# A graph network layer on one Trainium2 core: row beginnings by selection matrices, and the first count matrix made between the normalisations of x

## The chip, the cores and the metric

The kernel runs on one core of one Trainium2 chip. The time is device microseconds of one execution. Before the change the median of three runs is 3082.79 us (3079.99 to 3087.31). A profile is one further execution, taken by the hardware profiler; its own time stands beside it.

The engines are PE (matrix products; PEld is its weight load), DVE (vector), ACT (activations), POOL (GpSimd) and SP (issues DMAs). Each takes its instructions in order.

## The reference

6250 nodes with 256 features, and 100000 edges (src, dst), sorted by dst. x is normalised per row and clipped at zero, goes through four graph layers, and is added to the result:

```python
h = jnp.maximum(_layernorm(x, axis=-1), 0.0)
deg = segment_sum(ones, dst)
h = h @ W1_self + (segment_sum(h[src], dst) / clip(deg, 1)) @ W1_neigh + b1     # mean
hp = relu(h @ W2_pool + b2_pool)                                                # pool
h = h @ W2_self + segment_max(hp[src], dst) @ W2_neigh + b2
h = ((segment_sum(h[src], dst) + h) / (deg + 1)) @ W3_neigh + b3                # gcn
h = h @ W4_self + (segment_sum(h[src], dst) / clip(deg, 1)) @ W4_neigh + b4     # mean
return x + (h @ W_fc + b_fc)
```

dst is drawn as 6250 u^2, so the first nodes have many edges.

## The kernel before, in words

The nodes are 49 tiles of 128. Edges of tiles 8 to 48 are summed in `sums`: for each block of 128 edges one indirect DMA on POOL gathers 128 rows of a table (L379) into a ring of 14, a one-hot of the edges' node (`hot`, L375, DVE) is the weight of three matmuls (L397; a row is stored as three bf16 parts), and groups of four blocks are added to tiles on DVE (L414, L416). There are 474 such gathers in the first layer.

Tiles 0 to 7 (18 in later layers) have so many edges that they are done as a dense product with a **count matrix** A: how many edges lead from each node to each of the 128 nodes of the tile. `build` makes it from windows of 8 nodes. A window has up to 31 rows of 128 edges; for each row there is a one-hot of the source's place in its tile (`hs`, 128 x 128: two ACT activations, Abs at L303 and Relu at L305), a one-hot of tile and node (`hm`, 128 x 392, DVE, L307), and one matmul (L313); ACT evicts a window to fp8 (L317). Tile 0's matrix has 139 rows, tiles 1 to 7 have 322 together. `dense` multiplies it with the rows of all 49 tiles (L435, three matmuls each). `Hub` holds the pieces of matrices and dense products; `sums` takes from it in proportion to the gathers done, and one-hots are made up to four pieces ahead (`LOOK`), in rings of seven.

Ahead of the first layer stands the **preparation**:

- `load_x` and `layer_norm`: x in seven groups of seven tiles, in three buffers. DVE makes statistics (L567, L568), ACT normalises tile by tile (L577), and the group is split in three bf16 parts: first part by ACT (L580), subtraction on DVE (L581), second part by POOL (L582), subtraction on DVE (L583). SP stores it to `tab_h` (L584), which the gathers read.
- The first edge of each window of nodes. For 384 window bounds in three columns, a first lookup of rows of dst (`drow`, L614, one buffer, three in turn) and a count (L618) give the starts (`SN`). They are turned into one row by PE (`starts`), a check (`room`, `has`) is made, and POOL copies the starts in runs to the 896 rows of the matrices with 128 times the row's number added (`at_row`, L646 and L648, 33 runs). Seven small matmuls turn this back into columns (`atI`).
- `window_rows` looks up 128 dst and 128 src per row with `atI` (L669, seven times two indirect DMAs on POOL), and PE turns them (L679). `window_keys` makes the keys `sk` and `mk` from them on DVE (L686 to L695), for the first 512 rows (tiles 0 to 7) and later for the rest.
- `products1`: products of weights, in eight steps on PE and ACT. `turn` and `tail_keys`: the keys of the summed edges.

The order within an engine is made by a scheduler from the program's order and its dependencies, so that the work of these parts is interleaved. The first layer begins with `hub.advance(first)`, which makes the matrix of tile 0, and then `sums`. As each tile is complete, `done1` multiplies it with the weights (L815 to L838) and SP stores a tile of `tab_p` (L839). The second layer's gathers (L1137, POOL) read `tab_p` and begin once the last tile is stored.

Of the kernel before, what the change touches and what calls it, by code (L numbers as in the profile page):

```python
# [73 lines left out]
def fast_path(  # L74
# [216 lines left out]
    def build(d, A, keys, pool, psb):  # L291
# [3 lines left out]
        for w in range(d * WT, (d + 1) * WT):  # L295
            hold = {}
            for k in range(k_of[w]):
# [3 lines left out]
                def hot(r=r, hots=hots):  # L301
                    t = pool.tile([P, P], BF16, name="ht", bufs=3)
                    nc.scalar.activation(t, iota_b, AF.Abs, bias=sk[:, r : r + 1])  # L303
                    hots[0] = pool.tile([P, P], BF16, name="hs", bufs=LOOK + 3)
                    nc.scalar.activation(hots[0], t, AF.Relu, bias=one, scale=-1.0)  # L305
                    hots[1] = pool.tile([P, NT * WIN], BF16, name="hm", bufs=LOOK + 3)
                    nc.vector.tensor_scalar(hots[1], iota_w, mk[:, r : r + 1], None,  # L307
                                            op0=ALU.is_equal)
# [201 lines left out]
    for d in range(H1, NT):  # L510
        last = d == NT - 1
        ends = (g_of[d][0] * G * P, EX if last else (g_of[d][1] + 1) * G * P,
                offs[b_of[d][0]], EX if last else offs[b_of[d][1] + 1])
        for k in range(4):
            nc.gpsimd.memset(lim[:, k, d : d + 1], float(ends[k]))
# [8 lines left out]
    mk1 = w1pool.tile([P, RB1], F32, name="mk1")  # L524

    with ExitStack() as pro:
# [18 lines left out]
        def load_x(g):  # L545
            xt = lp.tile([P, LG, FI], F32, name="xt", bufs=3)
# [11 lines left out]
        for g in range(3):  # L558
            load_x(g)

        def layer_norm(g):
# [19 lines left out]
            nc.vector.tensor_sub(xt, xt, hi)  # L581
            nc.gpsimd.tensor_copy(mid, xt)  # L582
# [4 lines left out]
            )  # L587

# [22 lines left out]
        drows = dflat[0:EP].rearrange("(p t) -> p t", t=T)  # L611
        for c in range(3):
            row = ep.tile([P, T], I32, name="drow", bufs=1)
            nc.gpsimd.indirect_dma_start(  # L614
                out=row, out_offset=None, in_=drows,
                in_offset=bass.IndirectOffsetOnAxis(ap=cI[:, c : c + 1], axis=0),
            )
            nc.vector.tensor_scalar(row, row, SN[:, c, 1:2], 0.0, op0=ALU.is_lt, op1=ALU.add,  # L618
                                    accum_out=within[:, c : c + 1])
        nc.vector.scalar_tensor_tensor(SN[:, :, 0], cF, float(T), within,  # L620
                                       op0=ALU.mult, op1=ALU.add)
        pr_ = bank(psm, "pm", "pr_s", (3 * P,))
        for c in range(3):
            nc.tensor.matmul(pr_[:2, c * P : (c + 1) * P], SN[:, c, :], ident,
                             start=True, stop=True)
        starts = ep.tile([2, 3 * P], F32, name="starts")
        nc.vector.tensor_copy(starts, pr_[:2, :])


        room = ep.tile([1, NW], F32, name="room")  # L630
        i = 0
        while i < NW:
            n = sum(1 for w in range(i, NW) if k_of[w] == k_of[i])
            nc.gpsimd.memset(room[:, i : i + n], float(k_of[i] * P))
            i += n
        has = ep.tile([1, NW], F32, name="hasw")
        nc.vector.tensor_sub(has, starts[:1, 1 : NW + 1], starts[:1, :NW])
        nc.vector.tensor_tensor(has, has, room, op=ALU.is_gt)
        nc.vector.tensor_reduce(bad[:1, 1:2], has, AX.X, ALU.max)


        at_row = ep.tile([2, RB * P], F32, name="at_row")
        nc.gpsimd.memset(at_row, 0.0)
        nc.gpsimd.memset(at_row[:1, :], float(E))
        for r, w0, n, k in spans:
            nc.gpsimd.tensor_copy(at_row[:, r : r + n], starts[:, w0 : w0 + n])  # L646
            if k:
                nc.gpsimd.tensor_scalar(at_row[:1, r : r + n], at_row[:1, r : r + n],  # L648
                                        float(k * P), None, op0=ALU.add)
        pa = bank(psm, "pm", "pa", (RB, 2))  # L650
        for b in range(RB):
            nc.tensor.matmul(pa[:, b, :], at_row[:, b * P : (b + 1) * P], ident[:2, :2],
                             start=True, stop=True)
        atF = ep.tile([P, RB, 2], F32, name="atF")
        nc.vector.tensor_copy(atF, pa)
        atI = ep.tile([P, RB], I32, name="atI")
        nc.vector.tensor_copy(atI, atF[:, :, 0])


        sk = ep.tile([P, RB * P], F32, name="skf")  # L660
        mk = ep.tile([P, RB * P], F32, name="mkf")
        skI = ep.tile([P, RB * P], I32, name="skI")
        dw = ep.tile([P, RB * P], F32, name="dwf")

        def window_rows(b):
            got = []
# [13 lines left out]
            c = slice(b * P, (b + 1) * P)  # L680
# [3 lines left out]
        def window_keys(c0, c1):  # L684
            c = slice(c0, c1)
# [91 lines left out]
        turn()  # L777
        for b in range(RB1 // P):
            window_rows(b)
        window_keys(0, RB1)  # L780
        nc.vector.tensor_copy(sk1, sk[:, :RB1])
        nc.vector.tensor_copy(mk1, mk[:, :RB1])
        for g in range(NT // LG):
            layer_norm(g)
            if g + 3 < NT // LG:
                load_x(g + 3)
            next(steps, None)
            if RB1 // P + g < RB:
                window_rows(RB1 // P + g)
        for _ in steps:  # L790
# [1172 lines left out]
```

## Time and profile before

| what | value |
|---|---|
| median of three runs | 3082.79 us |
| the profiled execution | 3087.14 us, span 3085.3 us, granted clock 0.907 |
| busy PE, PEld | 2456.4 us (80%), 1401.4 us (45%) |
| busy DVE, ACT, POOL | 2053.6 (67%), 893.7 (29%), 2054.0 us (67%) |
| first gather of tab_h (L379) | 147.53 us |
| first gather of tab_p (L1137) | 820.96 us |
| L305 hs, all matrices | 781 of 395 ns mean |
| L307 hm with mk | 461 of 344 ns mean |
| L581, L583 subtractions | 7 of 2.02 us, 7 of 2.01 us mean |
| L582 cast on POOL | 7 of 1.76 us mean |

How to read it: a page gives busy time of each engine, and groups of instructions by line with the idle time just before them and what ended it ("<-"). In a timeline each row has the start and the duration in us from the span's start, the engine, the line, what is written from what, how many of them were merged ("x27"), and the idle time before. POOL's rows of an indirect DMA are its issue, not its transfer.

### The profile page before, as it was taken

What the parts mean: (1) busy time and instruction counts of PE and PEld (TensorE: products, weight loads), DVE (VectorE), ACT (ScalarE), POOL (GpSimd) and SP (SyncE); (2) the same over time, 40 slices, a digit from 0 to 9 for tenths busy, and PEclk for the clock granted to TensorE, in tenths of its full rate; (3) what the DMA queues carried; (4) which work ended last, traced back from release to release, by engine and by line L of the source; (5) the groups of instructions that cost most, each with busy time, mean ns of one, the idle gap of its engine ahead of it and who ended that gap; (6) DMA issues with size and microseconds to landing.
All of it is one profiled execution on the core that took longest, in us unless ns stands there. A gap on an engine that the chain in (4) does not pass through costs nothing. (4 is left out here: it accounts for less than half of the span.)

```text
span 3085.3 us, 41397 instructions
## 1 busy us (share of the span) xinstructions
PE 2456.4 (80%) x12699; PEld 1401.4 (45%) x12699; DVE 2053.6 (67%) x5303; ACT 893.7 (29%) x2383; POOL 2054.0 (67%) x2260
## 2 busy tenths in 40 slices
PE   1568999999768555666789997972899899799997
PEld 0234666666433222232334443431344344688786
DVE  4955666655367677555789997974466667576665
ACT  2557766664255566311111111000000001000000
POOL 5274777776366776777667777764676677677663
PEclk9777999999889777788899998985999999899999
DMA  5454667776599999999989998976999999777774
GB/s 190 152 159 138 203 208 211 213 217 211 196 392 376 362 388 352 362 389 384 314 274 324 315 309 296 323 248 210 361 387 373 364 386 382 254 225 219 208 210 135
DMA packets 379984, 865.38 MB, mean 280 GB/s; under 512 B 58064, under 2 KB 151202, under 8 KB 379720
## 3 DMA queue, kind: packets, MB, share of 16 engines
q0 software_dynamic: 146560, 514.74, 50.7%
q1 hardware_dynamic: 175108, 292.47, 25.6%
q10 hardware_dynamic: 58084, 55.44, 5.6%
q8 instruction: 103, 1.69, 0.2%
q14 instruction: 129, 1.06, 0.1%
HBM read 610.65 MB, written 252.58 MB: 280 GB/s over the span
## 5 line engine op out<-in xcount | busy, mean ns | idle before, releaser
L1137 POOL DMA_INDIRECT X<-tab_p,srcIf x782 | 842.3, 1077 | 368.6 <-issue 170.5
L397 PE MATMUL pg<-ring,hot 128*128 128x256 bf16 (+2 forms) x3390 | 685.9, 311 | 96.2 <-DMA ring<-tab_h,srcT 36.5
L435 PE MATMUL pd<-zt,ac 128*128 128x256 bf16 (+1 forms) x3462 | 569.9, 300 | 36.3 <-DMA ac<-tab_a 31.1
L379 POOL DMA_INDIRECT ring<-tab_h,srcT x474 | 450.7, 951 | 194.3 <-PE pg L397 72.2
L397 PEld LDWEIGHTS <-hot 128*128 128x128 bf16 x3390 | 334.2, 99 | 332.1 <-issue 163.4
L435 PE MATMUL pd<-r,ae 128*128 128x512 bf16 x1536 | 383.4, 399 | 102.9 <-DVE acc L934 46.9
L379 POOL DMA_INDIRECT ring<-tab_r,srcE x342 | 333.0, 974 | 162.2 <-PE pg L397 72.5
L435 PEld LDWEIGHTS <-ac 128*128 128x128 fp8e4 x3462 | 338.8, 98 | 171.3 <-DMA ac<-tab_a 23.9
L379 POOL DMA_INDIRECT ring<-tab_s,srcE x314 | 297.7, 948 | 130.2 <-PE pg L397 49.4
L1142 DVE SCALAR_TENSOR_TENSOR X<-X,samef,X 128x512 f32<-128x512 f32 x385 | 288.3, 749 | 133.2 <-DMA X<-tab_p,srcIf 90.9
L416 DVE SCALAR_TENSOR_TENSOR acc<-pg,M,acc 128x257 f32<-128x257 f32 (+2 forms) x518 | 274.7, 561 | 150.6 <-PE pg L397 150.3
L1142 DVE SCALAR_TENSOR_TENSOR X<-X,samef 128x512 f32<-128x512 f32 x391 | 293.1, 750 | 114.2 <-DMA X<-tab_p,srcIf 108.0
L313 PE MATMUL pb<-hm,hs 128*128 128x392 bf16 x781 | 256.2, 376 | 132.4 <-ACT A L317 66.4
L305 ACT ACTIVATE hs<-ht,onef 128x128 bf16<-128x128 bf16 x781 | 290.2, 395 | 240.9 <-PE pb L313 221.9
L435 PEld LDWEIGHTS <-ae 128*128 128x128 fp8e4 x1536 | 156.4, 102 | 338.9 <-issue 198.8
L1219 DVE TENSOR_SCALAR_CACHE_REDUCE many<-ac 128x896 bf16<-128x896 fp8e4 (+2 forms) x144 | 138.7, 963 | 132.7 <-DMA ac<-tab_a 132.7
L1076 PE MATMUL pm_prf<-unf,hTf 128*128 128x512 f32 x392 | 203.9, 647 | 16.6 <-ACT hTf L1067 16.6
L375 DVE TENSOR_SCALAR hot<-iota_bf,keyE 128x128 bf16<-128x128 bf16 x656 | 151.2, 274 | 72.5 <-PE pg L397 65.4
L307 DVE TENSOR_SCALAR hm<-iota_w,mk 128x392 bf16<-128x392 f16 x461 | 155.2, 344 | 56.7 <-PE pb L313 55.0
L317 ACT ACTIVATE A<-pb 128x392 fp8e4<-128x392 f32 x288 | 139.8, 489 | 182.0 <-PE pb L313 137.7
L435 PE MATMUL pd<-Z,A 128*128 128x256 bf16 (+1 forms) x1176 | 187.4, 274 | 0.2
L313 PEld LDWEIGHTS <-hs 128*128 128x128 bf16 x781 | 81.4, 105 | 217.7 <-issue 89.2
(288 smaller groups left out, 2908.1 us busy)
## 6 DMA issues: line engine op xcount, KB each, us to landing
runb<-X SPq DMA_DIRECT2D x208, 512.0 KB
runb<-X SPq DMA_DIRECT2D x183, 256.0 KB
tab_r<-r SPq DMA_DIRECT2D x49, 384.0 KB
tab_a<-A SPq DMA_DIRECT2D x18, 784.0 KB
tab_t<-th SPq DMA_DIRECT2D x49, 256.0 KB
tab_p<-hpf SPq DMA_DIRECT2D x49, 256.0 KB
th<-tab_t ACTq DMA_DIRECT2D x49, 256.0 KB
X<-tab_p,srcIf POOLq DMA_INDIRECT x782
```

The costliest lines, as they stand in the source:

```text
L305: nc.scalar.activation(hots[0], t, AF.Relu, bias=one, scale=-1.0)
L307: nc.vector.tensor_scalar(hots[1], iota_w, mk[:, r : r + 1], None, op0=ALU.is_equal)
L313: nc.tensor.matmul(hold[0], hots[0], hots[1], start=(k == 0), stop=(k == k_of[w] - 1))
L317: nc.scalar.copy(A[:, :, c : c + WIN], hold[0].rearrange("p (s c) -> p s c", c=WIN), saturate=True)
L375: nc.vector.tensor_scalar(hot[j], iota_b, keyT[:, j - jb : j - jb + 1], None, op0=ALU.is_equal)
L379: nc.gpsimd.indirect_dma_start(out=ring[:, j % deep, : 3 * F], out_offset=None, in_=table, in_offset=bass.IndirectOffsetOnAxis(ap=srcT[:, ...
L397: nc.tensor.matmul(pg[:, : F + c], hot[j], X[:, part * F : (part + 1) * F + c], start=(k == 0 and part == 2), stop=(k == n - 1 and part == 1),
L416: nc.vector.scalar_tensor_tensor(acc[d], pg, m, acc[d], op0=ALU.mult, op1=ALU.add)
L435: nc.tensor.matmul(hold[0][:, : F + c], a, z[:, part * F : (part + 1) * F + c], start=(s == ss[0] and part == 2), stop=(s == ss[-1] and pa ...
L1076: nc.tensor.matmul(pm, hT[:, c, :], un[:, c, :], start=False, stop=(c == KH - 1))
L1137: nc.gpsimd.indirect_dma_start(out=X[:, k, :], out_offset=None, in_=tab_p, in_offset=bass.IndirectOffsetOnAxis(ap=srcI[:, t : t + 1], axis=0),
L1142: nc.vector.scalar_tensor_tensor(X[:, k, :], prev, same[:, t : t + 1], X[:, k, :], op0=ALU.mult, op1=ALU.max,)
```

## The change

It has five parts. (1) The starts are no longer turned into a row. `win_of` holds for each of the 896 rows the number of its window (33 iotas on POOL), `select` makes of it three matrices with a one where the row's window is the partition's (DVE), and a matmul of `SN` with such a matrix, plus one of `later` (128 times the row's number) with a unit row, gives the beginnings as columns. The beginnings of tiles 0 to 7 need the first lookup of dst alone; `drow` has two buffers. (2) The check moves behind the second normalisation, and the fills of `lim` behind `turn`. (3) The keys of tiles 0 to 7 are made in place. (4) In `layer_norm`, the first subtraction moves from DVE to POOL and the second cast from POOL to ACT; x has two buffers in place of three. (5) The matrix of tile 0 is made in shares between the normalisations (`made.advance`), with its `hs` by one POOL instruction each; the other matrices keep ACT's. The first layer's Hub begins without it.

```diff
@@ build @@
-    def build(d, A, keys, pool, psb):
+    def build(d, A, keys, pool, psb, other=False):
...
                 def hot(r=r, hots=hots):
-                    t = pool.tile([P, P], BF16, name="ht", bufs=3)
-                    nc.scalar.activation(t, iota_b, AF.Abs, bias=sk[:, r : r + 1])
                     hots[0] = pool.tile([P, P], BF16, name="hs", bufs=LOOK + 3)
-                    nc.scalar.activation(hots[0], t, AF.Relu, bias=one, scale=-1.0)
+                    if other:
+                        nc.gpsimd.tensor_scalar(hots[0], iota_b, sk[:, r : r + 1], 0.0,
+                                                op0=ALU.add, op1=ALU.is_equal)
+                    else:
+                        t = pool.tile([P, P], BF16, name="ht", bufs=3)
+                        nc.scalar.activation(t, iota_b, AF.Abs, bias=sk[:, r : r + 1])
+                        nc.scalar.activation(hots[0], t, AF.Relu, bias=one, scale=-1.0)
@@ before the preparation @@
+    As = [bpool.tile([P, NT, P], F8, name="A0", bufs=1)]
+    made = Hub(build(0, As[0], (sk1, mk1, 0), bpool, psb1, other=True))
@@ load_x, layer_norm @@
-            xt = lp.tile([P, LG, FI], F32, name="xt", bufs=3)
+            xt = lp.tile([P, LG, FI], F32, name="xt", bufs=2)
...
             nc.scalar.copy(hi, xt)
-            nc.vector.tensor_sub(xt, xt, hi)
-            nc.gpsimd.tensor_copy(mid, xt)
+            nc.gpsimd.tensor_sub(xt, xt, hi)
+            nc.scalar.copy(mid, xt)
             nc.vector.tensor_sub(lo, xt, mid)
@@ beginnings @@
+        for r, w0, n, k in spans:
+            nc.gpsimd.iota(win_of[:, r : r + n], pattern=[[1, n]], base=w0,
+                           channel_multiplier=0, allow_small_or_imprecise_dtypes=True)
+            nc.gpsimd.memset(later[:, r : r + n], float(k * P))
...
+        def select(c):
+            nc.vector.tensor_scalar(sel[c], win_of[:, sel_at[c] : sel_at[c] + sel[c].shape[1]],
+                                    float(-c * P), pidx, op0=ALU.add, op1=ALU.is_equal)
...
-        for r, w0, n, k in spans:
-            nc.gpsimd.tensor_copy(at_row[:, r : r + n], starts[:, w0 : w0 + n])
-            if k:
-                nc.gpsimd.tensor_scalar(at_row[:1, r : r + n], at_row[:1, r : r + n],
-                                        float(k * P), None, op0=ALU.add)
...
+        def row_begins(b0, b1, cs):
+            pa = bank(psm, "pm", "pa", (RB, 2))
+            for b in range(b0, b1):
+                for c in cs:
+                    nc.tensor.matmul(pa[:, b, :], sel[c][:, b * P - sel_at[c] : (b + 1) * P - sel_at[c]],
+                                     SN[:, c, :], start=(c == cs[0]), stop=False)
+                nc.tensor.matmul(pa[:, b, :], later[:, b * P : (b + 1) * P], unit,
+                                 start=False, stop=True)
+            nc.vector.tensor_copy(atF[:, b0:b1, :], pa[:, b0:b1, :])
+            nc.vector.tensor_copy(atI[:, b0:b1], atF[:, b0:b1, 0])
@@ the order of the preparation @@
         steps = products1()
-        turn()
+        begins(0, 1)
+        row_begins(0, RB1 // P, (0,))
         for b in range(RB1 // P):
             window_rows(b)
-        window_keys(0, RB1)
-        nc.vector.tensor_copy(sk1, sk[:, :RB1])
-        nc.vector.tensor_copy(mk1, mk[:, :RB1])
+        window_keys(sk1, mk1)
+        select(1)
+        select(2)
+        begins(1, 3)
+        row_begins(RB1 // P, RB, (1, 2))
+        turn()
...
         for g in range(NT // LG):
             layer_norm(g)
-            if g + 3 < NT // LG:
-                load_x(g + 3)
+            if g + 2 < NT // LG:
+                load_x(g + 2)
             next(steps, None)
             if RB1 // P + g < RB:
                 window_rows(RB1 // P + g)
+            made.advance(len(made.work) * (g + 1) // (NT // LG + 2))
+            if g == 1:
+                check_room()
...
+        made.advance(len(made.work) * (NT // LG + 1) // (NT // LG + 2))
@@ the first layer @@
-        builds = [build(d, As[d % 2], keys, wk, psb) for d in range(H1)]
+        builds = [None] + [build(d, As[d % 2], (sk1, mk1, 0), bpool, psb1) for d in range(1, H1)]
...
-        work = list(builds[0])
-        first = len(work)
+        work = []
         for d in range(H1):
             work += merged(denses[d], builds[d + 1]) if d + 1 < H1 else denses[d]
+        made.advance(len(made.work))
         hub = Hub(work)
-        hub.advance(first)
         todo.append(segments())
```

## The prediction

> **What bounds the kernel now.** I read first the POOL timeline from 130 to 830 us, because the change ends where the first aggregation begins. Columns: start, duration, what, and in brackets the idle time before it and what ended it.
>
> ```profile
> 147.53 0.97 POOL L379 DMA_INDIRECT ring<-tab_h,srcT  x1 [9.24 <-DMA tab_h<-Z]
> ...
> 242.74 0.99 POOL L379 DMA_INDIRECT ring<-tab_h,srcT  x1 [0.30 <-PE pb L313]
> 244.04 0.95 POOL L379 DMA_INDIRECT ring<-tab_h,srcT  x1 [0.30 <-PE pb L313]
> 268.11 0.95 POOL L379 DMA_INDIRECT ring<-tab_h,srcT  x1 [23.13 <-PE pg L397]
> 272.69 0.94 POOL L379 DMA_INDIRECT ring<-tab_h,srcT  x1 [3.62 <-PE pg L397]
> ...
> 782.35 0.94 POOL L379 DMA_INDIRECT ring<-tab_h,srcT  x1 [0.71 <-PE pg L397]
> 820.96 0.97 POOL L1137 DMA_INDIRECT X<-tab_p,srcIf  x1 [37.66 <-DMA tab_p<-hpf]
> ```
>
> The first gather waits for the last tab_h store, so the preparation ends at S = 147.5. The next stage's first gather (L1137) waits for the last tab_p row, at 821.0. Everything later stands behind that gather, so a shift of it passes to the end one for one: the kernel is as long as S, plus this stage, plus an unchanged rest. The stage lasts 673.4 us. Gathers are issued every 1.25 us, so 474 of them take 591; there is one hole of 27 us at 244 to 273, where the ring is full because PE, in order, sits in the first count matrix; and at the end PE is behind. The windows view shows the latter (PE busy, PEld, DVE, ACT, POOL, granted clock, DMA share, GB/s):
>
> ```profile
> 200.00:250.00 50.00, 32.71 (x132) 14.28 (x130) 28.21 (x99) 35.22 (x116) 34.23 (x36) 0.70 0.51 147
> 600.00:650.00 50.00, 49.74 (x321) 32.91 (x320) 28.34 (x106) 31.67 (x84) 38.10 (x40) 1.00 0.73 223
> 700.00:750.00 50.00, 49.87 (x333) 34.21 (x332) 27.79 (x98) 28.11 (x72) 33.84 (x37) 1.00 0.68 200
> ```
>
> POOL's 40 gathers per 50 us (its pace) fall to 37 once PE has no idle time left. From 200 to 250 PE has time, at clock 0.70: there it waits for one-hots from ACT.
>
> The preparation is read from the whole timeline, 38 to 76 us:
>
> ```profile
> 40.21 2.75 POOL L646 COPY at_row<-starts 2x128 f32<-2x128 f32 x4 [3.03 <-DVE starts L627]
> 47.70 7.38 POOL L648 TENSOR_SCALAR at_row<-at_row 1x19 f32<-1x19 f32 x27
> 58.45 3.81 POOL L669 DMA_INDIRECT wrow<-dflat,atI  x1 [0.66 <-DVE nb L575]
> 58.93 2.01 DVE L583 TENSOR_TENSOR Z<-xt,Z 128x1792 bf16<-128x1792 f32 x1
> ```
>
> POOL makes the row beginnings in 62 small instructions, 40 to 56 us, and the row lookups (L669) start only at 58.5.
>
> **The change, part by part.**
>
> *Row beginnings (earlier by 31).* Removed: three chained lookups before anything, the 62 POOL instructions, the transposition. Added ahead of them on POOL: 33 iotas and 33 fills over 782 elements. An iota of 392 takes 0.45 us and one of 1 takes 0.13, the 164 fills of lim 5.5 in all; that gives about 5 us of iotas and fills, after win_of is cleared on DVE at about 4. The lim fills still stand ahead of the first dflat lookup in the built order: 4.4 + 5 + 0.5 + 5.5 = 15.4, against 13.3 before. Its data took 6.9 us from issue, so 22.3; then DVE 1.03 + 0.16, eight small matmuls at 0.3, two copies with a 1.03 us count between them: row lookups at 27.3 in place of 58.5. From lookup to finished keys (L694) before took 32.6 us with casts and subtractions of x in between; without these, some 25: keys at 52.5 in place of 91.
>
> *First count matrix (moved off the stage, onto POOL).* Its 139 one-hot pairs, matmuls and 16 evictions leave the stage. On ACT a pair (Abs, Relu) cost 1.17 us for two. On POOL each is one TENSOR_SCALAR with a pointer scalar and two operations; the trace has the same kind with one operation. POOL's groups by form, mean ns behind the busy time:
>
> ```profile
> L582 POOL CAST Z<-xt 128x1792 bf16<-128x1792 f32 x7 | 12.4, 1764 | 41.0 <-DVE xt L581 41.0
> L648 POOL TENSOR_SCALAR at_row<-at_row 1x1 f32<-1x1 f32 x17 | 3.4, 198 | 1.3
> L648 POOL TENSOR_SCALAR at_row<-at_row 1x128 f32<-1x128 f32 x1 | 0.6, 554 | 0.0
> ```
>
> So 2.8 ns per element plus 0.2; I take 0.55, and 0.62 with the gap of 0.07 that the run of 27 shows. Below: 0.38, if it runs like POOL's copy of 160 elements (0.31 + 0.07). Above: 0.98, if the second operation doubles the per-element part.
>
> Here a rule of the Trainium skill speaks against the change. DVE makes the other one-hot (L307) at the same time, from the same engine port. The rows where the two meet before:
>
> ```profile
> 136.42 1.87 POOL L582 CAST Z<-xt 128x1792 bf16<-128x1792 f32 x1 [1.67 <-DVE xt L581]
> 136.68 2.89 DVE L307 TENSOR_SCALAR hm<-iota_w,mk 128x392 bf16<-128x392 f16 x6
> 141.42 3.55 DVE L307 TENSOR_SCALAR hm<-iota_w,mk 128x392 bf16<-128x392 f16 x15
> ```
>
> Fifteen alone take 3.55 (0.24 each); six begun beside POOL's cast take 2.89 in place of 1.42, and 58.45 above shows the other direction: a POOL lookup of 0.94 takes 3.81 beside DVE's two-input subtraction. The skill ("SBUF — State Buffer", section "SBUF: two separate sides") says why: VectorE and GpSimd arbitrate for one port pair, which is locked for the whole instruction, the loser waiting. By it a one-hot pair costs 0.62 + 0.24 = 0.86, not 0.62. By the row alone the 119 one-hots ahead of the fifth subtraction take 74 us, by the rule 102; the first would turn my sum to a gain of 12. I take the rule, as the trace shows both directions.
>
> *x's subtraction to POOL, the cast to ACT.* POOL has no two-input row. Below: its one-input cast, 1.7 us; above: the TENSOR_SCALAR slope, 0.2 + 1792 x 2.8 ns = 5.2. The skill ("GPSIMD Engine Reference", section "3.1 Elementwise — side-by-side cycle accounting") gives 4497 ns for 2048 elements with two inputs: an estimate of 3.9, taken as 4.0, against 2.0 on DVE (L581) now. The cast is 1.7 on either engine.
>
> *One x buffer less.* The load of group g+2 now waits on SP until group g's last subtraction is done, about 8 us from release to use (the first load: issued 2.3, used 9.6). It hides behind one-hots for groups 2 to 4. It doesn't for 5 and 6: in DVE's built order group 5's scale (nb) stands behind group 4's last subtraction, and group 6's statistics behind eleven more one-hots. SP's last tab_h store also stands behind the matrix's own store, which waits for the last eviction; it is ready by then.
>
> *S, along POOL's queue.* One-hots start at 52, behind the first two subtractions (groups 0 and 1, 39 to 51, between the later lookups). In order then: 119 one-hots, 102.3; two lookups, 2.5; subtractions of groups 2 and 3, 8; about 5 for statistics and subtractions on DVE that the seven buffered one-hots don't cover. That is 170. Group 4: subtraction 4.0, cast 1.7, last subtraction 2.0; group 5: seven normalisations 3.6, cast 1.7, subtraction 4.0 (187); four one-hots ahead of it and group 6's statistics, 10; normalisations and casts 5.5 (the last 19 one-hots end at 203.5); subtraction 4.0, cast 1.7, subtraction 2.0 (211). From the last store to the first gather 6.0, as between 141.56 and 147.53 now. S = 217: 69.5 later. The one-hots, which lay beside the gathers, are on the path here; what hid them is gone.
>
> *The stage.* Gathers 473 x 1.25 = 591.3 with no hole (27 less). PE's work per gather: 853 pieces over 474 gathers become 714, 1.80 to 1.51; a piece is 0.33 us (three matmuls of 0.11) or 0.165, mean 0.255: 0.075 less. The last 99 gathers took 132 us now, 1.40 on PE's side with its backlog; 1.33 leaves a backlog of about 8 to 10. Behind the last gather now come 38.6 us, of which PE needs 23 to catch up; without backlog 19, with it 29. Stage: 620 against 673.4, **53 saved** (from 37, the hole and half of the rest, to 60).
>
> Sum: 69.5 - 53 = +16.5. The profiled execution is 3087.1 (span 3085.3 and 1.8 around it), 4.3 above the median; its sum is 3103.6, and against the median 3082.8 it gives **3099**.
>
> **The rivals.**
>
> 1. *Faster.* POOL's one-hot costs under 0.5 a pair, for instance 0.38 with DVE's part inside its dispatch gap. At 0.5 the 119 save 43: S = 174, time 3082.8 + 26.5 - 53 = **3056**. For it: the copy row, and that 0.2 of the 0.55 is fixed and perhaps holds no port. Against: the TENSOR_SCALAR rows and the two collisions. It decides from a pair under 0.72 (16.5/119 = 0.14 below 0.86).
> 2. *Costs and gains cancel* at a pair of 0.67 to 0.77, within 6 us of **3083**.
> 3. *Slower by more.* Two operations cost as two: pair 0.98 + 0.24 less some overlap, say 1.09; 119 x 0.23 = 27 more: **3126**. The same comes if the stage does not save its second half (only the hole, 27).
> 4. *It doesn't do what it says*: if the late end is PE's alone and its backlog stays, the stage saves 37, and the time is 3115; this lies inside the first case's range.
>
> **How the numbers follow.** 0.2% is 6 us, about what a measurement of this kernel tells from no change. My case (a pair near 0.86): 0.50, own range 3090 to 3118. Faster: 0.27. Cancelling: 0.10. Slower by more: 0.13. So faster 0.27, same 0.10, slower 0.63. The range leaves out a tenth on each side: below, pairs under 0.46 (3050); above, pairs over 1.19 (3138).
>
> **What would show it.** Row lookups at 27 and keys near 52. POOL's one-hots at 0.55 each but 0.86 from start to start, DVE's L311 lengthened beside them. POOL's subtraction near 4.0. The first tab_h gather near 217 (wrong if before 195). No hole of 23 us in the gathers; from the first to L1178's first gather 620. If the one-hots come every 0.6 or less, the lock does not bind and the prediction falls on the slow side; if POOL waits for ACT or x between one-hots, my account of the queue does.

## The result, and the profile after

The changed kernel takes 3101.75 us (median of five runs, 3098.83 to 3108.68); the kernel before, run beside it, 3082.79 (3076.58 to 3089.72). The ratio is 1.0062, with a 95% interval of 1.004 to 1.0084: slower by 19 us. The forecast was 3099.

| us | before | forecast | after |
|---|---|---|---|
| row lookups (L669, now L698) begin | 58.45 | 27.3 | 30.29 |
| keys of tiles 0 to 7 ready | 91.5 | 52.5 | 55.6 |
| one-hots of the first matrix begin | 134.46 | 52 | 54.54 |
| first gather of tab_h, S | 147.53 | 217 | 208.06 |
| last gather of tab_h | 782.35 | | 802.86 |
| first gather of tab_p | 820.96 | 837 | 839.67 |
| stage, between the two first gathers | 673.4 | 620 | 631.6 |
| span | 3085.3 | 3101.8 | 3106.8 |

POOL's timeline of the changed kernel, with the gathers that bound the stage (columns as before: start, duration, what, idle time before it):

```profile
208.06 1.05 POOL L383 DMA_INDIRECT ring<-tab_h,srcT  x1 [10.89 <-DMA tab_h<-Z]
...
802.86 0.95 POOL L383 DMA_INDIRECT ring<-tab_h,srcT  x1 [0.30 <-issue]
...
839.67 0.94 POOL L1178 DMA_INDIRECT X<-tab_p,srcIf  x1 [35.86 <-DVE hm L311]
```

The first gather waits for the last store of tab_h still, 60.5 us later than before. The hole of 23 us is gone: all further waits of the 474 gathers above their usual 0.30 us come to 1.6 us. The 36 us ahead of the first tab_p gather are nearly as they were (37.66).

Busy time of the engines in three stretches of it (PE, PEld, DVE, ACT, POOL, then granted clock, DMA share, GB/s):

```profile
200.00:250.00 50.00, 34.92 (x215) 21.01 (x213) 31.72 (x156) 31.30 (x102) 31.89 (x34) 0.90 0.53 155
650.00:700.00 50.00, 49.85 (x333) 33.92 (x332) 29.61 (x109) 29.48 (x75) 37.82 (x41) 1.00 0.70 207
750.00:800.00 50.00, 49.85 (x338) 34.68 (x338) 22.60 (x82) 14.41 (x30) 36.79 (x39) 1.00 0.74 222
```

PE is full in the later two, as it was, and POOL keeps up 39 to 41 gathers per 50 us beside it. So PE's backlog is carried to the end instead of holding gathers back. How long that is, the order of PE's matmuls shows (three for each gather): the last gather's end 20.5 us behind its issue (802.86 to 823.31; 22.3 before), those of the 200th gather 4.0 us behind.

```profile
822.82 0.49 PE L401 MATMUL pg<-ring,hot 128*128 128x257 bf16 x3
```

POOL in the preparation, from its timeline:

```profile
30.29 0.95 POOL L698 DMA_INDIRECT wrow<-dflat,atI  x1 [2.16 <-DVE mv L571]
...
54.54 6.93 POOL L304 TENSOR_SCALAR hs<-iota_bf,sk 128x128 bf16<-128x128 bf16 x7 [0.99 <-DVE sk L725]
...
64.01 35.17 POOL L304 TENSOR_SCALAR hs<-iota_bf,sk 128x128 bf16<-128x128 bf16 x47
...
115.76 8.71 POOL L304 TENSOR_SCALAR hs<-iota_bf,sk 128x128 bf16<-128x128 bf16 x12 [1.26 <-PE pb L317]
...
127.87 30.68 POOL L304 TENSOR_SCALAR hs<-iota_bf,sk 128x128 bf16<-128x128 bf16 x39
158.52 3.47 POOL L584 TENSOR_TENSOR xt<-xt,Z 128x1792 f32<-128x1792 f32 x1
```

From 54.5 to 158.5 POOL hardly rests (a single wait of 1.26 us in it, and gaps of some tenths), so its queue sets when the fifth subtraction of x (L584) can run: 158.5, with 119 of the 139 one-hots ahead of it. And the groups by form from 50 to 200 us, mean ns behind the busy time, then the idle time before them:

```profile
L304 POOL TENSOR_SCALAR hs<-iota_bf,sk 128x128 bf16<-128x128 bf16 x139 | 112.3, 825 | 11.3 <-PE pb L317 10.0 <-DVE sk L725 1.0
L311 DVE TENSOR_SCALAR hm<-iota_w,mk 128x392 bf16<-128x392 f16 x149 | 61.8, 458 | 21.8 <-PE pb L317 21.5
L584 POOL TENSOR_TENSOR xt<-xt,Z 128x1792 f32<-128x1792 f32 x6 | 21.4, 3571 | 0.9 <-ACT Z L583 0.9
```

One-hots on POOL start every 0.75 us in the first long run (35.17 for 47) and every 0.79 in the second (30.68 for 39). Their shortest, median and longest, in ns, and one place where they meet a subtraction of x on DVE (L586):

```profile
L304 POOL TENSOR_SCALAR hs<-iota_bf,sk x139: 704/714/2686, 54.5 to 192.9; 128x128 bf16<-128x128 bf16 x139
65.42 8.73 POOL L304 TENSOR_SCALAR hs<-iota_bf,sk 128x128 bf16<-128x128 bf16 x10
68.67 2.01 DVE L586 TENSOR_TENSOR Z<-xt,Z 128x1792 bf16<-128x1792 f32 x1
```

Ten at the usual 0.69 would take 6.9 us; the 1.8 more are about the length of the one subtraction beside them. So the mean of 825 ns is made by a few long ones: together the 139 are 16.9 us above 0.704 each, of which 13.2 lie in the 23 that overlap a DVE instruction with two tensor inputs, and 3.3 in the 80 that overlap DVE's `hm` alone (0.04 each). It is alike on DVE: `hm` takes 0.38 beside a one-hot of POOL's and 0.31 without, and the five that met POOL's subtraction took 2.9 on the mean, which makes most of the way from 344 ns before (in the whole kernel) to 458 here. DVE has idle time: it is busy 67.0 of the 98.5 us from 60 to 158.5.

In two groups of runs (e2, e7, e10 and e13; e7b, e14 and e15) the kernel before took 3459.8 and 3487.4 us, and the first layer's gathers waited 217 to 265 us beyond their usual 0.30 (1.6 in the changed kernel above, 41 in the kernel before), for a reason that the traces don't show, so that of those runs no stage is compared, but only the preparation, the tail and the ratio to the kernel before.

### The profile page after: what moved, and what is told of

The parts are those of the page before. It is cut to its first block, busy times and chain, and to the rows that moved or that the text cites. A ratio compares the mean times of both kernels' runs of the same rounds, so it can differ in the third digit from the quotient of the medians.

```text
span 3106.8 us, 41383 instructions
## 1 busy us (share of the span) xinstructions
PE 2475.2 (80%) x12719; PEld 1405.7 (45%) x12719; DVE 2057.9 (66%) x5304; ACT 826.6 (27%) x2112; POOL 2161.3 (70%) x2399
## 5 line engine op out<-in xcount | busy, mean ns | idle before, releaser
L401 PE MATMUL pg<-ring,hot 128*128 128x256 bf16 (+2 forms) x3390 | 677.1, 309 | 115.6 <-DMA ring<-tab_h,srcT 57.2
L309 ACT ACTIVATE hs<-ht,onef 128x128 bf16<-128x128 bf16 x642 | 240.1, 395 | 231.6 <-PE pb L317 219.6
L311 DVE TENSOR_SCALAR hm<-iota_w,mk 128x392 bf16<-128x392 f16 x461 | 166.8, 378 | 34.2 <-PE pb L317 32.8
```

The costliest lines, as they stand in the source:

```text
L401: nc.tensor.matmul(pg[:, : F + c], hot[j], X[:, part * F : (part + 1) * F + c], start=(k == 0 and part == 2), stop=(k == n - 1 and part == 1),
```

## The experiments

The theory: S is the length of POOL's queue, 139 one-hots of 0.7 to 0.9 and subtractions; what the stage gives back is PE's share of the matrix. The rivals: DVE and POOL lose the time to each other at a shared access; or x's own chain sets S; or the end of the stage is PE's total work, which no order can better.

The whole series in one table. e4, e1, e6 and e3 ran together with the kernel before at 3088.34 us (eight runs), e16 with one at 3089.67 (nine). Where no stage is given, it can't be compared. The tail is the time from the last gather of tab_h to the first of tab_p.

| kernel | first gather | stage | tail | ratio (95%) |
|---|---|---|---|---|
| before | 147.53 | 673.4 | 38.6 | 1 |
| after | 208.06 | 631.6 | 36.8 | 1.0062 (1.004 to 1.0084) |
| e4: row beginnings and order alone | 129.82 | 672.9 | 38.6 | 0.9934 (0.9906 to 0.9962) |
| e1: hs on DVE | 171.58 | 631.0 | 36.6 | 0.9922 (0.9895 to 0.9948) |
| e6: subtraction on DVE | 195.15 | 630.2 | 36.5 | 3080.74 us, one run |
| e3: hm from PSUM | 206.25 | 631.8 | 36.8 | 3105.67 us, one run |
| e2: hs on ACT | 182.96 | | 37.4 | 0.995, one run |
| e10: e4, hs on DVE | 130.53 | | 38.6 | 0.9923 (0.9905 to 0.994) |
| e13: hs on DVE again | 170.17 | | 37.9 | 0.9891 (0.9872 to 0.991) |
| e14: hs half POOL, half DVE | 172.93 | | 37.9 | 0.9936 (0.9916 to 0.9956) |
| e7, e7b: pieces earlier | 207.50, 207.92 | | 27.9, 28.0 | 0.9975 (0.996 to 0.9991), 1.0006 (0.9986 to 1.0026) |
| e15: e14 and pieces earlier | 173.45 | | 26.4 | 0.9927 (0.9898 to 0.9955) |
| e16: hs on DVE and pieces earlier | 171.42 | 622.1 | 22.4 | 0.9895 (0.9876 to 0.9914) |

### e4: only the row beginnings

The first matrix goes back into the stage with ACT's one-hots; subtraction, cast and the three buffers of x are as before. What stays is the new way to the beginnings and the order of the preparation.

```diff
-            nc.gpsimd.tensor_sub(xt, xt, hi)
-            nc.scalar.copy(mid, xt)
+            nc.vector.tensor_sub(xt, xt, hi)
+            nc.gpsimd.tensor_copy(mid, xt)
...
-            made.advance(len(made.work) * (g + 1) // (NT // LG + 2))
...
+        work = list(builds[0])
+        first = len(work)
+        hub.advance(first)
```

> Only the row beginnings by selection matrices and the new order of the preparation; the first matrix is made in the first layer as before with ACT's one-hots, the subtraction on DVE, the cast on POOL, three x buffers. If the early beginnings are worth what I reckoned and only the move of the matrix ate it: row lookups near 30, first gather at 118 to 128 in place of 147.5, stage 673 with its hole of 23 us as before, time about 3058. If the preparation of before was set by the work on x and not by the beginnings: first gather 140 to 147, time 3076 to 3083.

Measured: 3071.18 us, S = 129.82, at most 2 us later than expected. The gathers of e4 in POOL's timeline:

```profile
129.82 0.97 POOL L383 DMA_INDIRECT ring<-tab_h,srcT  x1 [9.47 <-DMA tab_h<-Z]
...
250.03 0.94 POOL L383 DMA_INDIRECT ring<-tab_h,srcT  x1 [22.61 <-PE pg L401]
...
802.69 0.97 POOL L1175 DMA_INDIRECT X<-tab_p,srcIf  x1 [37.66 <-DMA tab_p<-hpf]
```

The hole is back (22.6 us), the stage is that of the kernel before, and 17.7 us of S are gained. So these parts of the change, the beginnings together with the new order, are a gain of 0.66%, and the rest of it costs about 1.3%: more than the whole loss.

### e1 and e13: the first matrix's hs on DVE

```diff
-                        nc.gpsimd.tensor_scalar(hots[0], iota_b, sk[:, r : r + 1], 0.0,
+                        nc.vector.tensor_scalar(hots[0], iota_b, sk[:, r : r + 1], 0.0,
```

> The changed kernel with the first matrix's 139 POOL one-hots (L304) made on DVE; nothing else differs. If POOL's queue of one-hots sets the end of the preparation (my theory): POOL loses 112 us of work, DVE gains 139 x 0.18 = 25, so that a pair costs 0.24 + 0.18 = 0.42 on DVE in place of 0.75 on POOL; the first gather of tab_h comes at 175 to 185 in place of 208, the stage behind it stays at 630, and the time is about 3075. If the chain of x (two buffers, and scales and statistics queued on DVE behind later subtractions) sets it: the first gather stays at 200 to 208, the time at 3095 to 3102. If DVE is then the bound: later than 208, above 3102.

Measured: S = 171.58, 36.5 earlier and a little below the 175 to 185 expected, 3062.59 us. POOL's timeline of e1 at the end of the preparation:

```profile
133.97 3.46 POOL L584 TENSOR_TENSOR xt<-xt,Z 128x1792 f32<-128x1792 f32 x1 [10.08 <-ACT Z L583]
151.54 4.88 POOL L584 TENSOR_TENSOR xt<-xt,Z 128x1792 f32<-128x1792 f32 x1 [14.11 <-ACT Z L583]
170.76 0.17 POOL L371 MEMSET ring<- 128x28 bf16 x1 [14.34 <-DVE hs L304]
171.58 1.01 POOL L383 DMA_INDIRECT ring<-tab_h,srcT  x1 [0.65 <-issue]
```

POOL now waits 10 to 14 us for x (ACT's first part, L583) ahead of each subtraction; in the changed kernel x waited for POOL. DVE has become the full engine: it is busy 107.9 of 111 us from 60 to 171, and the clearing of the gathers' ring (L371), last ahead of the first gather, waits for DVE's one-hots; x's last store was issued at 160.2 already. POOL's queue is shown as the cause of S in the changed kernel, and 36.5 us as its price against the next engine in line.

Between e4 and e1 nothing is gained: S is 41.8 later, the stage 41.9 shorter, and the first tab_p gather comes at 802.69 and 802.60. (The 8.6 us between their times lie behind that gather, where the traces that can be compared differ from 2253.6 us in e6 to 2269.1 in e4 without an edit there.) Even on the fastest engine for it, the first matrix costs in the preparation what it gives in the stage.

e13 was meant to split the one-hots, but picked the engine by the row's number in its window, which is read only once the loop has ended, so that all were made on DVE.

```diff
+                        (nc.gpsimd if k % 2 else nc.vector).tensor_scalar(hots[0], iota_b, sk[:, r : r + 1], 0.0,
```

> The changed kernel, but every second 128 x 128 one-hot of the first matrix (odd rows of a window) is made by DVE in place of POOL, with the same instruction. Theory (the length of an engine's queue sets the first gather): POOL's one-hots take half of 139 x 0.70 = 49 us, DVE's pairs 139 x 0.23 + 70 x 0.16 = 43 us; with subtractions neither is alone the limit, so the first gather comes at 150 to 168 (208 with all on POOL, 172 with all on DVE), the stage stays at 631, and the time is 3040 to 3060. Rival (the two engines' shared access to the memory is what costs): POOL's and DVE's one-hots lengthen each other as soon as both run, and the first gather comes at 175 to 200, no earlier than with all on DVE.

Measured: S = 170.17. It tells nothing of the split; it repeats e1.

### e6: x's subtraction back on DVE

```diff
-            nc.gpsimd.tensor_sub(xt, xt, hi)
+            nc.vector.tensor_sub(xt, xt, hi)
```

> The changed kernel with x's first subtraction back on DVE (L584 in place of POOL's, 2.0 in place of 3.5 us each); the second cast stays on ACT, the one-hots on POOL. If POOL's queue sets the end: POOL loses 7 x 3.5 us, five of them (17) behind the start of the one-hots, DVE's subtraction blocks some of it (2 us each, two SBUF inputs); first gather 195 to 200, about 10 earlier. If the chain of x on DVE sets it: unchanged or later, 205 to 215.

Measured: S = 195.15, 3080.74 us (one run). So moving the subtraction back wins 12.9 of the 60.5 us. Seven of 3.5 us would be 24.5. Part of the rest is lost because more of DVE's two-input instructions now meet POOL's one-hots: 32 of these do, which are 23.1 us above 0.704 each (13.2 for 23 in the changed kernel), and the mean rises to 896 ns. Another part is a matter of order on SP: x's last subtraction ends at 183.2, but its store is issued at 187.7, behind the first matrix's own store at 187.3, which waits for the last eviction. In the changed kernel the matrix's store was issued at 194.8, well ahead of x's at 201.6.

### e3: hm read from PSUM

DVE's one-hot `hm` of the first matrix compares an iota in PSUM in place of one in SBUF, so that only its write and the key are left in the memory that POOL uses. The edit also takes one PSUM buffer from the transpositions, and it hands out the matrix's last pieces ahead of the later keys (`window_keys`) in place of behind them.

```diff
+        psi = pro.enter_context(tc.tile_pool(name="psi", bufs=1, space=PSUM))
+        iota_p = bank(psi, "pi", "iota_p", (NT * WIN,))
+        nc.vector.tensor_copy(iota_p, iota_w)
...
-                    nc.vector.tensor_scalar(hots[1], iota_w, mk[:, r : r + 1], None,
+                    nc.vector.tensor_scalar(hots[1], iota_w if other is None else other, mk[:, r : r + 1], None,
```

> The changed kernel with DVE's one-hot of the first matrix (L311) made from a copy of iota_w that lies in PSUM, so that it reads nothing of SBUF but the key; one PSUM buffer less for the transpositions. It costs DVE more, about 0.55 each in place of 0.24. If the shared port costs little (what the changed kernel's trace suggests: 0.69 from one POOL one-hot to the next where DVE makes none, 0.75 where it makes one each): POOL's one-hots come every 0.69 all along, 119 of them save 7, and no L311 waits for POOL; first gather near 200. If POOL's own cost is 0.55 and the port adds 0.2: they come every 0.55 and the first gather is near 185. If DVE's time is the bound: as late as 208 or later, and one-hots wait for PE.

Measured: S = 206.25, 3105.67 us (one run). The two groups of e3 from 50 to 215 us, then x's stores (first and last start) and the clearing of the ring:

```profile
L304 POOL TENSOR_SCALAR hs<-iota_bf,sk 128x128 bf16<-128x128 bf16 x139 | 106.4, 784 | 20.4 <-PE pb L317 19.4 <-DVE sk L728 1.0
L311 DVE TENSOR_SCALAR hm<-iota_p,mk 128x392 bf16<-128x392 f32 x139 | 75.8, 616 | 0.0
...
L590 SPq DMA_DIRECT2D tab_h<-Z x7: 359/360/370, 57.6 to 176.2; - x7
...
205.47 0.12 POOL L371 MEMSET ring<- 128x28 bf16 x1 [5.58 <-DMA stash_k<-mkf]
```

POOL's one-hots take 5.9 us less in all (106.4 against 112.3): 0.04 each, not the 0.24 of the forecast's second term. Those that overlap DVE's `hm` and no two-input instruction (98 of them) are 1.0 us above 0.704 in all, 0.01 each in place of 0.04; the two-input ones still cost 9.9. So the run sizes what `hm` takes from POOL, and it is little. S can't be used for that. x's last store was issued at 176.2, 25 us earlier than in the changed kernel, as 25 one-hots now stand behind x's last subtraction on POOL, where none did. But the ring is cleared only at 205.47, behind the store of the later keys, which the edit moved behind the whole matrix. POOL also waits 20.4 us by way of PE, where DVE's one-hot costs 616 ns.

### e14: half on POOL, half on DVE

```diff
+                        (nc.gpsimd if r % 2 else nc.vector).tensor_scalar(hots[0], iota_b, sk[:, r : r + 1], 0.0,
```

> The changed kernel, but the first matrix's 128 x 128 one-hots are made by POOL for odd rows and by DVE for even ones. (The run with alternating rows of a window made all of them on DVE: the row's number was read only when the loop had ended.) Theory (the longest queue sets the first gather): with all on DVE that queue ends at 171.6; it loses 69 of 139 instructions of 0.16 to 0.25 us, 11 to 17 us, and gets back some 7 where the rest runs beside POOL; POOL's half is 69 x 0.69 = 48 us and seven subtractions of 3.5. First gather at 158 to 168, stage 631, ratio to the kernel before 0.987 to 0.991. Rival (shared access to the memory): what POOL takes off DVE comes back as longer DVE instructions, first gather at 170 to 185, ratio 0.992 to 0.997.

Measured: S = 172.93, ratio 0.9936: within what the rival gave. Splitting is no better than DVE alone. The groups of e14 from 50 to 215 us, and then the busy time from 60 to 173 us in three stretches:

```profile
L304 POOL TENSOR_SCALAR hs<-iota_bf,sk 128x128 bf16<-128x128 bf16 x69 | 71.9, 1057 | 11.2 <-PE pb L317 10.8 <-PE pt_m L864 0.2
L304 DVE TENSOR_SCALAR hs<-iota_bf,sk 128x128 bf16<-128x128 bf16 x70 | 28.3, 406 | 1.9 <-PE pb L317 1.9
```

```profile
60.00:100.00 40.00, 32.40 (x125) 14.40 (x126) 40.00 (x151) 17.34 (x29) 35.54 (x37) 0.98 0.50 154
100.00:140.00 40.00, 15.66 (x44) 4.13 (x42) 37.33 (x138) 17.16 (x27) 31.77 (x25) 0.59 0.40 128
140.00:173.00 33.00, 12.85 (x37) 4.49 (x38) 31.53 (x113) 14.17 (x29) 22.12 (x17) 0.50 0.33 124
```

DVE is busy 108.9 of 113 us, though half of the one-hots left it. Both engines' instructions are longer: DVE's one-hot takes 0.305 us beside one of POOL's (52 of them) and 0.243 beside none, and the 40 of POOL's that overlap DVE's one-hots and no two-input instruction are 0.27 us above 0.704, for 0.04 in the changed kernel. So a part of what is taken off the one engine does come back on both. The means alone say more than that: 406 ns on DVE (299 in e1) and 1057 on POOL are raised by a few instructions of up to 3.5 and 4.6 us that met the other engine's subtraction of x, and in e14 these few are divided among half as many. Nor is the sharing all that sets S. Here it is x's chain again, with its last store issued at 167.0 (160.2 in e1): POOL's last subtraction of x, behind POOL's own one-hots, comes at 159.57 for 151.54. The rival's number was met; how much of it is the sharing and how much POOL's queue ahead of the subtractions was not separated.

### e2: the one-hots on ACT, in the preparation

```diff
-    made = Hub(build(0, As[0], (sk1, mk1, 0), bpool, psb1, other=True))
+    made = Hub(build(0, As[0], (sk1, mk1, 0), bpool, psb1))
```

> The changed kernel, but the first matrix's one-hots are made by two activations each on ACT as in the kernel before, so that only their place (in the preparation) differs from it. Theory: the place costs, whichever engine has the longest queue; ACT has 139 x 1.17 = 163 us of them, 7 normalisations of 3.6 and casts, some 220 us in all, of which keys allow the start at 52: first gather 205 to 235, stage 631, time 3100 to 3130. Rival (POOL alone was the wrong engine, and ACT had room): first gather 150 to 180, time 3045 to 3075.

Measured: S = 182.96, between the two, nearer to the rival's range; one run, 3442.49 us against 3459.82. With ACT's two activations of 0.39 us each S is 25 us earlier than with POOL's one of 0.7 to 0.8, and DVE's `hm` stays at a mean of 337 ns beside them. But this is not the price of the whole matrix: x's chain ended first (last store issued at 177.0), 113 of the 139 one-hots stood ahead of the first gather, and the others were made until about 227, beside the gathers. What they cost there can't be read from this run.

### e10: e4, and the one-hots on DVE in the stage

```diff
-        builds = [build(d, As[d % 2], (sk1, mk1, 0), bpool, psb1) for d in range(H1)]
+        builds = [build(d, As[d % 2], (sk1, mk1, 0), bpool, psb1, other=d == 0) for d in range(H1)]
```

(with `other` on DVE, as in e1.)

> The kernel with the new row beginnings alone (first matrix in the first layer's stage, subtraction on DVE, cast on POOL, three x buffers), and in addition the first matrix's 128 x 128 one-hots by one DVE instruction each in place of two on ACT. Theory: the hole of 23 us in the gathers is there because ACT makes a pair of activations in 1.17 us; on DVE the two one-hots take 0.16 and 0.23 us, so the matrix is done before the ring fills: first gather 128 to 138, hole under 8, stage 640 to 655 in place of 672.9, time 3045 to 3058 (3071.2 with ACT). Rival: what the hole gives is lost again behind it, since PE is the limit of the whole stage; then the hole goes, but the stage stays at 665 to 675, and the time at 3065 to 3075. Other rival: the one-hots now stand ahead of x's chain on DVE; then the first gather moves to 145 to 160 and the sum gains nothing.

Measured: S = 130.53 as the theory had it, but the hole did not go: it moved. POOL's timeline of e10:

```profile
149.40 1.27 POOL L383 DMA_INDIRECT ring<-tab_h,srcT  x1 [0.30 <-issue]
150.97 1.27 POOL L383 DMA_INDIRECT ring<-tab_h,srcT  x1 [0.31 <-issue]
178.41 1.00 POOL L383 DMA_INDIRECT ring<-tab_h,srcT  x1 [26.18 <-PE pg L401]
```

DVE is busy 25.00 of 25.00 us in both stretches from 130 to 180, and PE makes the matrix's matmuls without one of a gather until 177.6: the ring is full after 14 gathers. The ratio (0.9923) can't be told from e4's (0.9934). A cheaper one-hot did not remove the hole. It stands where the matrix stands ahead of the gathers' matmuls on PE: in e4 the two were mixed and 78 gathers came before the hole, here 14.

### e7, e7b, e15 and e16: the pieces handed out 15% faster

```diff
-                    hub.advance(math.ceil(len(hub.work) * (at - wait) / (T - j0 - wait)))
+                    share = (at - wait) / (T - j0 - wait)
+                    hub.advance(math.ceil(len(hub.work) * min(1.0, share * (1.15 if counts else 1.0))))
```

> The changed kernel, but the pieces of the count matrices and dense products in the first layer are handed out 15% faster than in proportion to the gathers, so that none is left for the last eighth of them. Theory: at the end of the stage PE is behind because pieces are spread to the very end; then PE has its backlog earlier, beside gathers that POOL could have issued, or catches up before the end. If the pieces only lie badly, the time from the last gather to the second layer's first gather falls from 36.8 to under 28 us, the stage from 631.6 to 620 to 625, and the time to about 3092. Rival: PE is full from 600 us on and its total work is the limit; then the wait moves from the end to the middle (gathers wait longer for the ring between 600 and 750), the stage stays at 628 to 634 and the time within 4 us of the changed kernel's 3101.8. The first gather stays at 208 in both.

> The same kernel as in the run before it with this edit (pieces of matrices and dense products handed out 15% faster in the first layer), whose first layer ran there with pauses of 2 to 5 us of all engines, so that only the tail (27.9 us in place of 36.8) could be read from it. Theory: where gathers come every 1.25 us, the stage falls from 631.6 to 620 to 625 with a tail under 29, and the time is 0.2 to 0.4% below the changed kernel (ratio to the kernel before 1.002 to 1.004). Rival (PE's total work is the limit): gathers are held back by the full ring between 500 and 780 us by as much as the tail gives, stage 628 to 634, ratio 1.005 to 1.0075.

Measured: the tail falls to 27.9 and 28.0 us (36.8 without), as both explanations had it. The intervals of their ratios (to 0.9991, from 0.9986) barely meet, and the stage, which would tell the two apart, can't be read from them. The preparation is untouched, and its first gather repeats: 207.50 and 207.92 for 208.06. e15 (with e14's split) then gave a tail of 26.4 and a ratio that can't be told from e14's.

> The two edits before it together: odd rows' one-hots on POOL and even ones on DVE, and pieces handed out 15% faster in the first layer. If they add, the first gather comes at 158 to 168, the tail is under 29, the stage 620 to 625, and the ratio to the kernel before is 0.984 to 0.988; if PE's total work is the limit of the stage, it is that of the half-and-half kernel within 0.1%.

> The kernel with all of the first matrix's 128 x 128 one-hots on DVE, and in addition the pieces of matrices and dense products handed out 15% faster in the first layer. The first gather stays at 170 to 173 in any case. Theory (the pieces' place is what delays the end): tail under 29 in place of 36.6, stage 620 to 625 in place of 631.0, ratio to the kernel before 0.3% below that of the kernel without the second edit (0.9922 on the chip of the first runs, 0.9891 on another), so 0.986 to 0.990. Rival (PE's total work in the stage is the limit): tail under 29 as well, but the last gather later by as much, stage 628 to 634, ratio 0.989 to 0.994. If the engines pause on this chip as they did in the runs since the second call, only the tail and the ratio can be read.

Measured for e16: 3057.66 us (3053.12 to 3062.04), S = 171.42. POOL's timeline of e16:

```profile
771.06 0.95 POOL L383 DMA_INDIRECT ring<-tab_h,srcT  x1 [0.30 <-issue]
793.50 0.94 POOL L1179 DMA_INDIRECT X<-tab_p,srcIf  x1 [21.49 <-DVE hm L311]
```

The tail is 22.4 in place of 36.6, the last gather 5 us later (771.06 against 766.03 in e1), as gathers waited some 5 us for the ring between 680 and 730. Net: a stage of 622.1 in place of 631.0; the four kernels with the first matrix in the preparation and the pieces in proportion lie between 630.2 and 631.8. Busy time of e16, and then of e1, in the same two stretches:

```profile
300.00:400.00 100.00, 91.44 (x625) 63.02 (x625) 60.04 (x221) 67.32 (x182) 75.69 (x80) 0.98 0.66 198
700.00:760.00 60.00, 54.38 (x319) 33.98 (x318) 29.61 (x114) 12.16 (x22) 44.64 (x49) 0.97 0.72 215
```

```profile
300.00:400.00 100.00, 86.31 (x571) 58.98 (x570) 57.24 (x211) 60.95 (x161) 75.63 (x81) 0.97 0.67 198
700.00:760.00 60.00, 59.81 (x403) 41.28 (x401) 29.31 (x107) 21.76 (x49) 45.38 (x49) 1.00 0.75 224
```

PE takes 5 us more per 100 where it had idle time, and 5 less per 60 at the end. So the late end was a matter of where the pieces lay: the theory, not PE's total work. e16 has the lowest median of the kernels whose times can be compared, and beats both kernels: ratio 0.9895 to the kernel before. But against e1's 0.9922 the intervals overlap, and e13, which is e1's kernel again, had 0.9891; so the 9 us are shown for the stage, by the traces, and not for the whole time. e4 with the pieces earlier was not run.

## Why the prediction was right

The direction, the size (3099 forecast, 3101.75 measured) and the mechanism held: the one-hots, once beside the gathers, stand on POOL ahead of x's last groups, and cost more there than their leaving gives the stage. But the number came out closer than its terms did, which is luck.

- *Row beginnings.* 27.3 forecast, 30.29 measured: the first lookup was issued at 16.60 for 15.4, and a count of the next column and DVE's statistics came in between. (POOL's small instructions before were 64, not 62.) The one-hots begin 2.5 late. e4 shows what the beginnings and the new order are worth where x's chain sets S: 17.7 us, not the 28 by which the lookups moved.
- *The one-hot.* The step took 0.62 for its own pitch and the whole 0.24 of DVE's `hm` by the lock rule. Measured: 0.69 where DVE makes none, and over the 119 ahead of the fifth subtraction 93.4 us, 0.785 each. Its own part was undersized by 0.07 and the port's oversized by 0.14 (0.10 for 0.24); the second outweighs, and 102.3 became 93.4. The row (one operation from f32) was near, but two operations on bf16 cost a quarter more than its 0.55.
- *The lock.* This step had the wrong partner. The Trainium skill ("SBUF — State Buffer", section "SBUF: two separate sides") has the loser wait for the whole instruction where the DVE instruction runs in a two-port mode or has two inputs in SBUF; my step left that condition out and charged each `hm`, which has one tensor input, in full. In the trace the lock is seen where DVE has two inputs: of the 11.5 us by which the 119 one-hots exceed 0.704, 8.4 lie in the 17 that overlap such an instruction, one of them delayed by 1.98 us beside a subtraction of 2.01. The 69 beside `hm` alone make 2.9, 0.04 each for 0.24. Whether `hm` runs in a two-port mode the trace doesn't show. Why it costs POOL so little, while it takes 0.38 itself for 0.31, no run shows; the rival's own idea, that DVE's part falls in POOL's dispatch gap, would fit.
- *The subtraction.* 4.0 taken from an estimate of 3.9 by the Trainium skill ("GPSIMD Engine Reference", section "3.1 Elementwise — side-by-side cycle accounting"); 3.5 measured. Two ahead of the fifth: 6.9 for 8. The 5 us of waits were 1.3.
- *S.* Start +2.5, one-hots -8.9, subtractions -1.1, waits -3.7, and from the fifth subtraction to the first gather 49.5 for 47: together -9, so 208 for 217.
- *The stage.* The hole went as forecast, and e4 and e1 show that it is the matrix's (it returns and leaves with it). Forecast were 53 us, 41.8 came. The step that was mis-sized is the tail, 36.8 for 29, and in it the backlog with which PE enters the last 99 gathers, which I put at nothing. The saving per gather was right: in PE's own order the last 99 took 1.436 us each before and 1.362 after, 0.074 less for my 0.075 (my 1.40 was low: the last 99 gathers took 137.0 us before, not 132). So was the growth: gathers came every 1.270, which leaves 9.1 us over the 99, for my 8 to 10. But PE was then 11.4 us behind the gathers already, for 4.0 at the 200th: 7 us that the sum doesn't have. PE's busy time rises along the stage, as the pieces stay at 1.51 per gather but more and more are dense products (0.74 per gather from the 100th to the 200th, 1.10 in the last 99): 1.10 us per gather from the 100th to the 200th, then 1.21 to the 300th, 1.25 to the 375th and 1.36 to the end. It fell behind from the 200th on although 12.6 us of PE were still idle up to the 375th; what it waited for there was not looked into. The other 3.5 us of the stage are the gathers' own, 594.8 for 591.3. e16 agrees: with the pieces earlier PE is 9.8 us behind at the last gather in place of 20.5, and the tail is 22.4. That its stage is then 622, near the forecast, is chance.
- *The rest.* 2267.1 us from the first tab_p gather to the end against 2264.3: +2.8 where I had none; the traces that can be compared differ by up to 16 us there, so this is no effect of the change that could be told from nothing.

So -9 on S, +11 in the stage and +3 behind it: errors of opposite sign that nearly cancel. With the first two right (S 208, stage 632 as measured) the same sum gives 3101. The rival *faster* fell with the pair at 0.78, above its 0.72; *slower by more* needed 1.09; that costs and gains cancel, which asked for 0.67 to 0.77, was missed by little.

## What to carry to other kernels

Work that is taken out of a stage whose engines wait goes somewhere: reckon the queue of the engine that receives it up to the moment when the next stage may start, for each engine that could take it. Here the same one-hots put S at 172 on DVE and at 208 on POOL (at 183 on ACT, with a fifth of them left for the next stage), and even 172 only paid back what the stage won, while the earlier row beginnings and the new order alone were the gain. When an edit is used to size one effect, look at what the next stage's first instruction waits for: in e3, e6 and e14 it was not what the edit was meant to move. A backlog at the end of a stage is followed from the place where the slower engine begins to fall behind; here that was near the 200th of 474 gathers, and a sum over the last 99 missed 7 us. Handing pieces out somewhat early took 9 us off the stage in the pair of traces that shows it.

## What the runs showed of the hardware

- One comparison with two operations on 128 x 128 bf16 takes POOL 0.70 us at least, a pitch of 0.69 alone; DVE makes the same in a pitch of 0.16, ACT in two activations of 0.39.
- POOL's one-hots are delayed most by DVE instructions with two tensor inputs: in the changed kernel one of 0.70 us took up to 2.69 beside such an instruction. DVE's one-hot `hm`, 0.31 us alone, took up to 3.62 beside POOL's subtraction of 3.5 and, in the kernel before, 1.74 beside POOL's cast of 1.87. Beside the other engine's one-hots alone it was 0.04 more on POOL and 0.07 more on DVE; in e14, with DVE busy 108.9 of 113 us, 0.27 more on POOL.
- With x's first subtraction on DVE too (e6), 32 POOL one-hots in place of 23 overlapped a two-input instruction, and their mean was 896 ns in place of 825.
- POOL's DMA issue is touched too: 1.27 us in e10 (a gather every 1.58) while DVE made one-hots without a break, against 0.95 (every 1.25).
